# Attention weights summed over partitions by VectorE transpositions, and the first scores of an image spread evenly

## The chip, the cores and the metric

The kernel runs on one core of a Trainium2 chip. The metric is the time of one execution on the device, in microseconds (us); the time of a kernel is the median of its runs. TensorE (PE in the profile) multiplies matrices, VectorE (DVE) and ScalarE (ACT) work on tensors in SBUF and PSUM, GpSimd (POOL) on tensors in SBUF, and SyncE (SP) here issues transfers.

## The reference

Two layers on x of shape (4, 256, 64, 64) in float32. The first is attention over the 4096 positions of each image, with 32 channels for queries and keys:

```python
q = einsum('oc,bcn->bno', wq, xf) + bq
k = einsum('oc,bcn->bon', wk, xf) + bk[None, :, None]
attn = softmax(einsum('bnd,bdm->bnm', q, k), axis=-1)
v = einsum('oc,bcn->bon', wv, xf) + bv[None, :, None]
out = einsum('bcn,bmn->bcm', v, attn)
x = gamma[0] * out + x
```

The second layer is a cluster block: a group norm, a clustering of points around pooled centres with its own small projections, a second group norm, a two-layer perceptron with GELU (256 to 1024 to 256 channels), an affine step with ReLU, and a last 256 to 256 projection with ReLU. The change touches the attention alone.

## The kernel before, in words

The four images go one after the other. For each there are two long stages: `weighting` (the attention, some 525 us) and `cluster` with `mlp` (the second layer, some 328 us). The instructions of all engines are put out in one order written by hand, and each engine works through its own in that order.

In the attention an image's 4096 queries are cut into 8 blocks of 512 (`NBLK`), and for each block the 4096 keys into 8 groups of 512 (`GRP`). A pair of block `nb` and group `g` is a unit `u = 8 nb + g`; an image has 64 units. A unit goes through four steps:

- `score(u)` (L347): four float32 products give the scores of 512 keys by 512 queries, keys on the partitions, into the two double-bank PSUM tiles of `ps_s`. ScalarE copies both halves to SBUF (L377, L382) and VectorE takes running maxima of both (L381, L384; in the first group of a block L379 alone). Only two such tiles exist, so the next score waits until both have been read by both engines.
- `exps(u)` (L443): VectorE subtracts the maximum of each query (two instructions, L451), ScalarE takes the exponential (two, L454), GpSimd adds the weights to a running sum `acc` (two, L459; one, L456, for the first group).
- `weigh(u, av, quarter)` (L461), quarters 0 to 3: products of the weights with the values, accumulated over the block's eight units in the PSUM tiles `av`. These products at L464 fill most of TensorE's time. A float32 product shows as two records in the profile, so a quarter has 4 records and a unit 16.
- Once per block: `fold`, `highest` and `known` (the maximum of each query over the partitions, for the next block), `gather` (L473: the two halves of `acc` are added into `rdens`), `clear` (`av` is scaled out of PSUM), `total`, `add` (L498: GpSimd multiplies by the reciprocal sums and adds to the image), `seen` and `pooled` (statistics).

`highest` (L414) already gets from partitions to a row without TensorE: a VectorE transposition of 32 by 32 blocks (L417), a reduction (L420), four copies that bring the four groups of 32 partitions together (L423), a second reduction (L425), a small transposition (L428), and then `everywhere` (L81): one transfer of the row to HBM (L84) and one that reads it back to all 128 partitions (L85).

`total` (L483) does for the sums what `highest` does for the maxima, but with TensorE: four products with a matrix of ones (L488) give the sums on the partitions, VectorE takes the reciprocal of 128 by 128 numbers (L496), and the same two transfers spread them. It is called for block `nb - 1` in the first unit of block `nb`, between the products of quarters 1 and 2; seven times per image, 28 in all. The last block of an image has its own path (L645 to L672), which the change leaves alone.

What order the scores have against the products is in the table `at`, which maps (unit, quarter) to the unit whose scores come next. As a rule the scores of unit `u + 10` come at the start of unit `u` (`LEAD` is 10). For the second to fourth image, the first eight scores of its own stage have a rule of their own, since only units 0 to 7 have scores by then:

```python
at = {(u, 0): u + LEAD for u in range(units - LEAD)}
if b:
    for i in range(6):
        del at[i, 0]
    at.update({divmod(3 * i + 2, RG): GRP + i for i in range(8)})
```

Of the kernel before, what the change touches and what calls it, by code (L numbers as in the profile page):

```python
# [8 lines left out]
F32 = mybir.dt.float32  # L9
AF = mybir.ActivationFunctionType  # L10
ALU = mybir.AluOpType
AX = mybir.AxisListType

P = 128
# [3 lines left out]
NB = 512  # L18
NBLK = N // NB
XT = 1024  # L20
D = 32
# [7 lines left out]
RG, GRP = 4, N // NB  # L29
# [16 lines left out]
def attention_then_cluster_block(  # L46
# [17 lines left out]
    nc = tc.nc  # L64
# [7 lines left out]
    swap = ctx.enter_context(tc.tile_pool(name="swap", bufs=1))  # L72
# [4 lines left out]
    ps_m = ctx.enter_context(tc.tile_pool(name="ps_m", bufs=2, space=PSUM))  # L77

    dram = ctx.enter_context(tc.tile_pool(name="dram", bufs=2, space=bass.MemoryType.DRAM))

    def everywhere(dst, rows, shape, name):  # L81

        d = dram.tile([NB], F32, tag="row", name=f"row_{name}")
        nc.sync.dma_start(out=d.rearrange("(a b) -> a b", a=shape), in_=rows)  # L84
        nc.sync.dma_start(out=dst, in_=d.partition_broadcast(P))  # L85

    def load_x(b, t):
# [17 lines left out]
    for r in range(RG):  # L105
        nc.sync.dma_start(
            out=bqk_s[r * D : (r + 1) * D, :], in_=pv[:D, PV["bq"] : PV["bq"] + 2]
# [12 lines left out]
        out=pool_w[:, :, :16], in_=consts[:, K_POOL : K_POOL + P].rearrange("p (j s) -> p j s", j=8)  # L120
# [24 lines left out]
    ones = const.tile([P, P], F32, name="ones")  # L145
# [125 lines left out]
    def attention(b, xs):  # L271


        own = {}
        stats = small.tile([P, 2 * NBLK, 6], F32, tag="stats", name=f"st1_{b}")
        cells = small.tile([P, KC, NBLK, 4], F32, tag="cells", name=f"cells_{b}")
        qs, slots, mxs, accs, tops, rdens, ts = {}, {}, {}, {}, {}, {}, {}
# [128 lines left out]

        def spare():
            if "w2" not in own:
                own["w2"] = swap.tile([P, 3, P], F32, tag="w2", name=f"few_{b}")
                nc.gpsimd.memset(own["w2"], 0.0)  # L410
            return own["w2"]

        def highest(nb):

            top = tops.pop(nb)
            fl = top[:, 1]
            nc.vector.transpose(fl, top[:, 0])  # L417
            low = spare()[:, nb % 2]
            mx = low[:, :16]
            nc.vector.tensor_reduce(mx, fl.rearrange("p (c n) -> p c n", n=D), AX.X, ALU.max)  # L420
            four = low[:D, D : D + 64].rearrange("p (r c) -> p r c", r=4)
            for r in range(4):
                nc.vector.tensor_copy(four[:, r], mx[r * D : (r + 1) * D])  # L423
            one = low[:D, 3 * D : 4 * D]
            nc.vector.tensor_reduce(  # L425
                one[:, :16], low[:D, D : D + 64].rearrange("p (r c) -> p c r", r=4), AX.X, ALU.max
            )
            nc.vector.transpose(low[:D, :D], one)  # L428
            mb = work.tile([P, NB], F32, tag="w2", bufs=1, name=f"mr_{b}_{nb}")
            everywhere(mb, low[:16, :D], 16, f"mx_{b}_{nb}")  # L430
            return mb

        def known(nb, mb):
# [48 lines left out]

        def total(nb):  # L483


            den = ps_m.tile([P, NB], F32, tag="m", name=f"den_{b}_{nb}")
            for j in range(4):
                nc.tensor.matmul(  # L488
                    den[j * D : (j + 1) * D, :P],
                    ones[:, :D],  # L490
                    rdens[nb][:, j * P : (j + 1) * P],
                    start=True,
                    stop=True,
                )
            rec = spare()[:, 2]
            nc.vector.reciprocal(rec, den[:, :P])  # L496
            everywhere(rdens[nb], rec[::D], 4, f"rd_{b}_{nb}")

        def add(nb):
            t_s, rden = ts.pop(nb), rdens.pop(nb)  # L500
# [58 lines left out]
        at = {(u, 0): u + LEAD for u in range(units - LEAD)}  # L559
        if b:  # L560
            for i in range(6):
                del at[i, 0]
            at.update({divmod(3 * i + 2, RG): GRP + i for i in range(8)})
        else:
            at[0, 2], at[0, 0] = at[0, 0], GRP + 1

# [7 lines left out]
        def weighting(ahead, fill, early):  # L574
# [3 lines left out]
            for u in range(units):  # L578
# [29 lines left out]
                if nb:  # L608
                    if g == 0:
                        total(nb - 1)  # L610
                    elif g == 3:
                        add(nb - 1)
                    elif g == 5:
                        seen(nb - 1)
                    elif g == 7:
                        pooled(nb - 1)
# [5 lines left out]
                if g == GRP - 3 and more:  # L622
                    mb = highest(nb + 1)
# [724 lines left out]
    with tc.manual_schedule():  # L1348
        here = attention(0, xs0)
        here.alone()  # L1350
        late = None
        for b in range(B):
            xs1, begun = [], []
            nxt = attention(b + 1, xs1) if b + 1 < B else None

            def ahead():
                if nxt and len(xs1) < N // XT:
                    xs1.append(load_x(b + 1, len(xs1)))
                elif late and not begun:
                    begun.append(begin())  # L1360

            begin, todo, gelu = late or (None, list(nxt.projections) if nxt else [], lambda i: None)
            fill = filler(todo)
            stats, cells, rest = here.weighting(ahead, fill, (lambda: None) if b else derived)
            stats2 = cluster(b, here.xs, stats, cells, rest, fill, gelu)

            late = mlp(b, here.xs, stats2, fill, nxt, NBLK - (b == B - 2))
            here = nxt
# [76 lines left out]
```

## Time and profile before

| | |
|---|---|
| time, median of 3 runs | 3447.35 us (3444.46 to 3449.81) |
| span of the profiled execution | 3448.3 us |
| TensorE busy | 3390.0 us, 98% |
| VectorE busy | 2002.3 us, 58% |
| ScalarE busy | 1678.9 us, 49% |
| GpSimd busy | 1489.6 us, 43% |
| products of `total`, L488 | 224 records, median 285 ns each |
| products of `weigh`, L464 | 4096 records, 1831.5 us busy |
| products of `score`, L359 | 2048 records, 297.8 us busy |
| row of sums: transfer out, then back to all partitions | 1.3 us and 3.1 us to landing |

How to read it: the groups of instructions list, for each line and form, how often it ran, how long it was busy and what it waited for. Records of products overlap[...]; so a count times the mean of one overstates what they cost, and the chain of work that ended last, which gives every stretch of time to one piece of work, is the better measure of a cost in a stage that TensorE bounds. The waits list who sat idle for whom. The timeline gives start and length of single instructions, and shows how early a result is there before the engine that needs it asks for it.

### The profile page before, as it was taken

The numbers are of one execution on the slowest core, as the hardware profiler recorded it, in microseconds if no ns is written. First come the engines' busy times: TensorE is split into PE (matmuls) and PEld (weight loads), VectorE is DVE, ScalarE is ACT, GpSimd is POOL, SyncE is SP. The second block draws the span as 40 slices with busy tenths as digits, with TensorE's granted clock in tenths as the row PEclk, the third lists the DMA queues.
The fourth block names the chain that finished last, engine by engine and source line by source line (L and its number), as shares of the span: only waits on it lengthen the run. The fifth ranks groups of instructions, "written<-read, shape, count | busy, mean of one in ns | idle before, by whom it ended". The sixth has DMA issues, their size and how long they took to land.

```text
span 3448.3 us, 32176 instructions
## 1 busy us (share of the span) xinstructions
PE 3390.0 (98%) x11760; PEld 1673.2 (49%) x11760; DVE 2002.3 (58%) x2995; ACT 1678.9 (49%) x2157; POOL 1489.6 (43%) x807
## 2 busy tenths in 40 slices
PE   8999999999999999999999999999999999999999
PEld 4433445655433344565543343466553343446565
DVE  4666664645566666464456666646546666754543
ACT  5545543444555554344455555434445555543444
POOL 2665665211255666521125566652004566672200
PEclk9999999999999999999999999999999999999999
DMA  2000002000000000200000000020000000010000
GB/s 70 13 13 13 13 11 80 7 19 13 20 12 13 13 13 22 69 7 19 19 16 13 10 14 12 22 69 7 19 19 13 13 13 13 13 35 1 13 19 25
DMA packets 40829, 70.03 MB, mean 20 GB/s; under 512 B 8848, under 2 KB 16224, under 8 KB 40672
## 3 DMA queue, kind: packets, MB, share of 16 engines
q1 hardware_dynamic: 35808, 61.16, 5.4%
q10 hardware_dynamic: 4608, 6.30, 0.8%
q8 instruction: 93, 1.52, 0.2%
q14 instruction: 64, 0.52, 0.1%
q0 software_dynamic: 256, 0.52, 0.0%
HBM read 42.68 MB, written 16.89 MB: 17 GB/s over the span
## 4 chain that ended last, share of the span: by engine, by line
PE 94%; DVE 4%; ACT 1%; issue 1%; DMA 0%; SPq 0%; ACTq 0%; DVEq 0%
PE av L464 52%; PE mo L1202 12%; PE sc L359 8%; PE hu L1195 4%; PE pw L1171 3%; PE hp L1195 3%; PE hq L1195 3%; PE vp L310 2%; PE fv L857 2%; PE op L978 1%; PE qp L329 0%; PE kp L287 0%; PE agg L887 0%; DVE vf L866 0%; DVE hs L1231 0%
## 5 line engine op out<-in xcount | busy, mean ns | idle before, releaser
L464 PE MATMUL av<-s,v 128*128 128x512 f32 x4096 | 1831.5, 600 | 0.6 <-ACT s L454 0.6
L459 POOL TENSOR_TENSOR acc<-acc,s 128x1024 f32<-128x1024 f32 x448 | 1056.5, 2358 | 558.7 <-ACT s L454 539.7
L464 PEld LDWEIGHTS av<-s,v 128*128 128x128 f32 x4096 | 758.6, 190 | 1039.9 <-issue 1031.6
L454 ACT ACTIVATE s<-s 128x1024 f32<-128x1024 f32 x512 | 539.9, 1057 | 527.2 <-DVE s L451 486.1
L451 DVE TENSOR_TENSOR s<-s,mb 128x1024 f32<-128x1024 f32 x512 | 595.0, 1205 | 16.8 <-ACT mb L435 15.1
L381 DVE TENSOR_TENSOR top<-sc,top 128x1024 f32<-128x1024 f32 x196 | 239.8, 1223 | 473.5 <-PE sc L359 473.5
L1202 PE MATMUL mo<-hs,w 128*128 128x512 f32 x992 | 507.7, 595 | 3.8 <-ACT hs L1224 1.6
L1224 ACT ACTIVATE hs<-hs,pv_s 128x256 f32<-128x256 f32 x496 | 251.4, 508 | 359.9 <-DVE hs L1231 348.9
L1231 DVE TENSOR_TENSOR hs<-hu,hs 128x256 f32<-128x256 f32 x372 | 157.5, 423 | 355.4 <-ACT hs L1234 205.6
L377 ACT COPY s<-sc 128x1024 f32<-128x1024 f32 x224 | 225.3, 1006 | 283.9 <-PE sc L359 283.8
L1157 POOL TENSOR_TENSOR xn<-xn 128x256 f32<-128x256 f32 x27 | 23.9, 887 | 682.0 <-DVE xn L1144 459.8
L359 PE MATMUL sc<-q,k 32*128 32x512 f32 x2048 | 297.8, 640 | 6.8 <-ACT s L382 6.8
L384 DVE TENSOR_TENSOR top<-sc,top 128x1024 f32<-128x1024 f32 x196 | 240.0, 1225 | 50.4 <-ACT s L377 35.2
L382 ACT COPY s<-sc 128x1024 f32<-128x1024 f32 x224 | 227.0, 1013 | 71.6 <-DVE top L379 36.1
L456 POOL TENSOR_TENSOR acc<-s 128x1024 f32<-128x1024 f32 x32 | 75.3, 2353 | 364.2 <-ACT s L454 364.2
L1231 DVE TENSOR_TENSOR hs<-hq,hs 128x256 f32<-128x256 f32 x372 | 146.0, 420 | 107.1 <-PE hq L1195 102.9
L1202 PEld LDWEIGHTS mo<-hs,w 128*128 128x128 f32 x992 | 186.6, 190 | 42.5 <-ACT hs L1234 7.8
L359 PEld LDWEIGHTS sc<-q,k 32*128 32x128 f32 x2048 | 83.0, 183 | 199.9 <-issue 136.6
L1195 PE MATMUL hp<-xn,w 128*128 128x256 f32 x496 | 150.6, 385 | 2.6 <-ACT v L318 2.6
L1195 PEld LDWEIGHTS hp<-xn,w 128*128 128x128 f32 x496 | 92.4, 190 | 72.9 <-issue 62.4
L310 PE MATMUL vp<-wv_s,x 128*128 128x256 f32 x512 | 123.4, 387 | 0.2 <-ACT v L318 0.2
L1171 PE MATMUL pw<-xn,wpw_s 128*128 128x512 f32 x248 | 112.0, 594 | 3.4 <-ACT xn L1265 2.2
(219 smaller groups left out, 2696.7 us busy)
## 6 DMA issues: line engine op xcount, KB each, us to landing
x<-in_x SPq DMA_DIRECT2D x32, 512.0 KB, 5.8
out<-xn SPq DMA_DIRECT2D x62, 256.0 KB, 2.1
w<-in_w SPq DMA_DIRECT2D x8, 1024.0 KB, 9.7
mr<-row_mx SPq DMA_DIRECT2D x28, 256.0 KB, 3.1
rden<-row_rd SPq DMA_DIRECT2D x28, 256.0 KB, 3.1
q<-q ACTq DMA_DIRECT2D x96, 64.0 KB, 2.0
mix<-in_wfv SPq DMA_DIRECT2D x8, 192.0 KB, 4.9
q<-q SPq DMA_DIRECT2D x24, 64.0 KB, 2.0
```

Source lines behind the costliest of these rows:

```text
L359: nc.tensor.matmul(halves[r // 2][:, r % 2, :], k_s[rows, g, :], q_s[rows, :], start=True, stop=True)
L381: nc.vector.tensor_tensor(top, halves[1], top, ALU.max)
L382: nc.scalar.copy(s[:, 2:4, :], halves[1])
L384: nc.vector.tensor_tensor(top, halves[0], top, ALU.max)
L451: nc.vector.tensor_tensor(sh, sh, mxs[nb].unsqueeze(1).to_broadcast([P, 2, NB]), ALU.subtract)
L454: nc.scalar.activation(sh, sh, AF.Exp)
L459: nc.gpsimd.tensor_tensor(acc, acc, s[:, 2 * h : 2 * h + 2], ALU.add)
L464: nc.tensor.matmul(av[c], own["v"][:, RG * g + quarter, c * P : (c + 1) * P], slots[u][:, quarter, :], start=(g == 0 and quarter == 0), st ...
L1195: nc.tensor.matmul(out, w[:, j * P : (j + 1) * P], x, start=True, stop=True)
L1202: yield nc.tensor.matmul(acc[c], w2_s[:, jj, c * P : (c + 1) * P], hs[:, i], start=(j == 0 and i == 0), stop=(j == HID // P // 2 - 1 and i ...
L1224: nc.scalar.activation(dst, src, act, bias=bias)
L1231: nc.vector.tensor_tensor(dst, ps, term, ALU.add)
```

## The change

`total` gives up the four products and the PSUM tile. It sums over partitions as `highest` takes maxima: what both do is put into `reduced` (block transposition, reduction, four copies, second reduction; the operation is an argument) and `rows` (small transposition and the two transfers). The reciprocal is then taken of 32 by 16 numbers, ahead of the small transposition. The scratch tile of `spare` grows from three to seven parts for the transposed sums; only the first three are cleared, as before. The row of sums leaves from 16 partitions rather than 4. The purpose is to take this work off TensorE.

The second edit is to the table `at`: the first eight scores of the second to fourth image's stage come at quarters 2, 4, 7, 10, 13, 16, 18 and 21 of the stage rather than at 2, 5, 8, 11, 14, 17, 20 and 23. The next score after them is at quarter 24 in both. The purpose is to have no two scores closer than two quarters.

```diff
-    def everywhere(dst, rows, shape, name):
+    def everywhere(dst, rows, name):
         d = dram.tile([NB], F32, tag="row", name=f"row_{name}")
-        nc.sync.dma_start(out=d.rearrange("(a b) -> a b", a=shape), in_=rows)
+        nc.sync.dma_start(out=d.rearrange("(a b) -> a b", b=D), in_=rows)
         nc.sync.dma_start(out=dst, in_=d.partition_broadcast(P))
...
-                own["w2"] = swap.tile([P, 3, P], F32, tag="w2", name=f"few_{b}")
-                nc.gpsimd.memset(own["w2"], 0.0)
+                own["w2"] = swap.tile([P, 7, P], F32, tag="w2", name=f"few_{b}")
+                nc.gpsimd.memset(own["w2"][:, :3], 0.0)
...
+        def reduced(src, flipped, low, op):
+            nc.vector.transpose(flipped, src)
+            nc.vector.tensor_reduce(
+                low[:, :16], flipped.rearrange("p (c n) -> p c n", n=D), AX.X, op
+            )
             four = low[:D, D : D + 64].rearrange("p (r c) -> p r c", r=4)
             for r in range(4):
-                nc.vector.tensor_copy(four[:, r], mx[r * D : (r + 1) * D])
+                nc.vector.tensor_copy(four[:, r], low[r * D : (r + 1) * D, :16])
             one = low[:D, 3 * D : 4 * D]
             nc.vector.tensor_reduce(
-                one[:, :16], low[:D, D : D + 64].rearrange("p (r c) -> p c r", r=4), AX.X, ALU.max
-            )
+                one[:, :16], low[:D, D : D + 64].rearrange("p (r c) -> p c r", r=4), AX.X, op
+            )
+            return one
+
+        def rows(one, low, dst, name):
             nc.vector.transpose(low[:D, :D], one)
+            everywhere(dst, low[:16, :D], name)
...
         def total(nb):
-            den = ps_m.tile([P, NB], F32, tag="m", name=f"den_{b}_{nb}")
-            for j in range(4):
-                nc.tensor.matmul(
-                    den[j * D : (j + 1) * D, :P],
-                    ones[:, :D],
-                    rdens[nb][:, j * P : (j + 1) * P],
-                    start=True,
-                    stop=True,
-                )
-            rec = spare()[:, 2]
-            nc.vector.reciprocal(rec, den[:, :P])
-            everywhere(rdens[nb], rec[::D], 4, f"rd_{b}_{nb}")
+            few = spare()
+            low = few[:, 2]
+            flipped = few[:, 3:].rearrange("p a n -> p (a n)")
+            one = reduced(rdens[nb], flipped, low, ALU.add)
+            nc.vector.reciprocal(one[:, :16], one[:, :16])
+            rows(one, low, rdens[nb], f"rd_{b}_{nb}")
...
-            at.update({divmod(3 * i + 2, RG): GRP + i for i in range(8)})
+            at.update({divmod((14 * i + 10) // 5, RG): GRP + i for i in range(8)})
```

## The prediction

> **What bounds the kernel now.** I read the page first: the busy time of the engines and the chain of work that ended last.
>
> ```profile
> PE 3390.0 (98%) x11760; PEld 1673.2 (49%) x11760; DVE 2002.3 (58%) x2995; ACT 1678.9 (49%) x2157; POOL 1489.6 (43%) x807
> PE 94%; DVE 4%; ACT 1%; issue 1%; DMA 0%; SPq 0%; ACTq 0%; DVEq 0%
> ```
>
> TensorE is busy for 98% of the span and holds 94% of the chain. So work taken off TensorE counts in full as long as nothing else then makes it wait, and work put on VectorE (58% busy) counts only where it makes TensorE wait. What is worth asking is what the four sums cost TensorE, where it idles, and how much time VectorE has around them. For the first, the chain in order of time around the first sums of the first image:
>
> ```profile
> 134.40 3.63 PE av L464 x8
> 138.03 0.36 PE den L488 x8
> 138.39 3.63 PE av L464 x8
> 142.02 1.07 PE sc L359 x8
> 143.09 7.06 PE av L464 x16
> ```
>
> The columns are start, length and work; in a timeline a bracket gives the idle time before and who ended it. The sums hold 0.36 us of the chain, and their mean of 285 ns times 8 records (2.28 us) would be six times too much. But the unit that they split takes 3.63 + 3.63 = 7.26 us for its 16 products where the next takes 7.06: breaking the run of products costs another 0.20 us. The distance between the starts of successive scores says the same: 142.02 - 133.33 = 8.69 us with the sums, 150.15 - 142.02 = 8.13 without, 0.56 us more. The same distances stand around the sums of another image (987.26, 995.95, 1004.08 in the timeline).
>
> For the second, the chain through the first eight units of the second image, from its first products at 915.28 to the products of its unit 7:
>
> ```profile
> 963.64 1.14 PE sc L359 x8
> ...
> 977.44 1.13 PE sc L359 x4
> 978.57 1.83 PE av L464 x2
> ```
>
> Between the first two lines the chain leaves TensorE: it goes over VectorE's maxima of the score at 963.64, the fold and `highest`, the subtraction, and ScalarE's exponential and copies, and only comes back with the second half of the score at 977.44. The cause is in the table of scores: quarters 23 and 24 each have one, one quarter of products apart. For the price I add up the stretch as if TensorE had not waited, from pieces of the same answer: the first 8 products 3.43, seven runs of 12 at 5.35 = 37.45, a run of 4 at 1.92 (a run of n costs 0.20 + 0.43 n, which fits 3.63, 5.35 and 7.06), a run of 16 at 7.06, ten scores at 1.07 = 10.70. That is 60.56 us; it took 978.57 - 915.28 = 63.29. So 2.73 us are lost. The waits name only 0.50 + 0.78 = 1.28 us of it (for ScalarE's copy L382); the rest sits inside records that were issued and then stood. The third and fourth image show the same 63.29 (1770.69 to 1833.98, 2601.27 to 2664.56). The first image has no such rule and no such wait.
>
> **What the Trainium skill says.** "VectorE: DVE Perf Modes", section "The three transpose paths": VectorE transposes only blocks of 32 by 32. That is why the change needs four copies across groups of 32 partitions and a second reduction; the trace has the same sequence in `highest`, so I take its durations and not the page's. "PSUM — Partial Sum Buffer", section "PSUM bank collisions raise a hardware error": two engines must not touch one bank and quadrant at a time, two readers included. The trace agrees: ScalarE's copy L382 waits 0.25 us for VectorE's L381 on the same half, and L384 waits for L377. So each score is given back only after two rounds, which matters for the replay below. "TensorE: Matmul & The Clock Gate", section "Part 3: Packing small matmuls": products in different column groups run at the same time. The sums use four column groups, and 8 records of 285 ns in 0.36 us agree.
>
> **The change part by part.** Removed from TensorE: 28 times 0.56 = 15.6 us (bounds: 0.36 if the 0.20 stays behind elsewhere, 10.1 us, to 0.56).
>
> Added to VectorE, from these groups of instructions (busy time, then mean of one in ns):
>
> ```profile
> L496 DVE RECIPROCAL few<-den 128x128 f32<-128x128 f32 x28 | 26.6, 949 | 4.2 <-PE den L488 4.2
> L417 DVE STREAM_TRANSPOSE top<-top 128x512 f32<-128x512 f32 x28 | 19.5, 696 | 0.1
> L420 DVE TENSOR_REDUCE few<-top 128x16 f32<-128x512 f32 x28 | 19.2, 686 | 1.2
> L423 DVE COPY few<-few 32x16 f32<-32x16 f32 x112 | 18.3, 164 | 2.1
> L425 DVE TENSOR_REDUCE few<-few 32x16 f32<-32x64 f32 x28 | 6.9, 248 | 1.0
> L428 DVE STREAM_TRANSPOSE few<-few 32x32 f32<-32x32 f32 x28 | 5.6, 199 | 1.0
> ```
>
> New per block: 0.696 + 0.686 + 4 x 0.164 + 0.248 + 0.199 = 2.49 us, and a reciprocal of 16 columns. That size is not in the trace; reciprocals of 1 and 64 columns take 160 and 553 ns, so 16 columns lie between, and on the line 160 + 6.24 x 15 = 0.25 us (bounds 0.16 to 0.55). Sum 2.74, less 0.95 for the old reciprocal: 1.8 us more busy. With the gaps that the sequence shows in `highest` (1034.12 to the next subtraction at 1036.71, 2.59 us) and 0.28 for the reciprocal, the stretch is 2.87 us where the old one was 0.86 (993.54 to 994.40): VectorE comes 2.0 us later to what follows, 56 us over 28 blocks, 1.6% of the span.
>
> Does that reach TensorE? Behind the sums on VectorE stand the subtractions for the next unit but one, then the maxima of the next score; ScalarE's exponentials wait for the first, and its copies stand behind these. TensorE waits for two things: weights and a free score tile. From the timeline of the second image:
>
> ```profile
> 993.54 0.95 DVE L496 RECIPROCAL few<-den 128x128 f32<-128x128 f32 x1
> 994.40 2.28 DVE L451 TENSOR_TENSOR s<-s,mb 128x1024 f32<-128x1024 f32 x2
> 995.95 1.14 PE L359 MATMUL sc<-q,k 32*128 32x512 f32 x8
> 998.71 1.22 DVE L384 TENSOR_TENSOR top<-sc,top 128x1024 f32<-128x1024 f32 x1 [0.30 <-ACT s L377]
> 1004.08 1.14 PE L359 MATMUL sc<-q,k 32*128 32x512 f32 x8
> ```
>
> Replayed 2.0 later: subtractions from 996.4 to 998.7, exponentials to 999.8, L381 to 999.9, copies L377 to 1000.8 and L382 to 1001.8, L384 to 1002.0. The next score now wants the tile at 1004.08 - 0.56 = 1003.5: 1.5 us to spare. Those exponentials are needed only by the products behind that score, 4.8 us later. After that score VectorE has caught up: in the old timeline it idles 3.12 us before the maxima that follow. So I cost the added 56 us of VectorE at nothing; a longer reciprocal (0.55) would still leave 1.2 us.
>
> The new first instruction reads `rdens`, which GpSimd's `gather` has written at 979.3, 14 us before: no new wait. The row of sums leaves 2.0 us later, after 996.4, and takes 1.3 and 3.1 us to land plus issue, so it is back near 1001.3; GpSimd asks for it at 1014.97. The larger scratch tile, the freed PSUM tile and the row from 16 partitions (as the row of maxima has it) have nobody waiting on them.
>
> The scores: with the new quarters the stretch costs, by the same pieces, 3.43 + 2 x 3.63 + 6 x 5.35 + 7.06 + 10.70 = 60.55 us if nobody waits. The replay of it, score by score: where two quarters lie between (quarters 2 to 4, and 16 to 18) the next score comes 4.7 us after the one before it. The first pair is the tightest: the score at 918.71 is read out by L382 at 923.2, as in the trace, and its tile's second half is wanted near 923.9. The second pair: score at 949.1, L384 to 952.9, wanted at 953.8. The score at quarter 21 (960.2) is read by 963.8, `highest` ends at 967.3, the exponentials of unit 7 at 970.6, wanted at 975.8; the next unit's first score, at 966.6, is off its tile at 973.9, wanted at 974.8. So no wait is left, and 3 x 2.73 = 8.2 us come back (bounds: 3 x 1.28 = 3.8 if only the named waits do).
>
> Sum: 15.6 + 8.2 = 23.8 us, and 3447.35 - 23.8 = 3423.6 us.
>
> **The rivals.** One: the gain is partial. The 0.20 us stays where other work splits the products, or the closer pairs of scores wait for ScalarE as the old pair did: 10.1 + 3.8 = 13.9 us, 3433.4. For it speaks that the margin of the first pair is only 0.7 us; against it, that the distances between scores measure the 0.56 directly.
>
> Two: the wait moves. VectorE's 2.0 us per block uses more than the 1.5 us to spare, by about what is saved, and TensorE waits some 0.8 us per block: 28 x 0.8 = 22.4, 3446. This needs my replay to be 1.3 us too early.
>
> Three, slower: VectorE sets the pace at the start of each block, so all of its 2.0 us show: 28 x 2.0 = 56 against 23.8 gained, +32, 3480. For it speaks only that the chain does run over VectorE where two scores lie close; against it, VectorE's idle time of 473.5 us before L381, for scores from TensorE.
>
> **How the numbers follow.** Forecast as worked out 0.72, rival one 0.16, two 0.06, three 0.06. The time is that of the first case. For the range I add the scatter of the time before (3 us) below, 3420, and on the other side take in rival one and its scatter, 3437; rivals two and three, 0.12, stay outside. Faster by over 0.2% (under 3440.5): 0.88. Same: 0.06. Slower: 0.06.
>
> **What would show it right or wrong.** In the changed kernel successive scores around the new sums lie 8.13 us apart, like their neighbours; the second image goes from its first products to those of unit 7 in 60.6 us; TensorE has no wait for L382 or L384 after the sums; VectorE's busy time grows by about 50 us; and GpSimd's `add` has no wait for the row of sums. A wait of TensorE on the score tile two scores after a block begins would make rival two or three true. A stretch above 62 us at the start of an image would say that the even spacing only moved the wait.

## The result, and the profile after

The changed kernel takes 3418.46 us (median of 4 runs, 3414.81 to 3419.37) against 3445.9 us for the kernel before: a ratio of 0.9918, 95% interval 0.9901 to 0.9935. Five later runs gave 3418.48 us and 0.9914 (0.9900 to 0.9928). It is faster, as forecast, but by more: the forecast was 23.8 us less and a range that ended at 3420.0. In the mean the two kernels are 28.3 us apart in the first comparison (four runs of each) and 30.3 us in the second (26 runs of the kernel before, five of the changed one).

The page of the changed kernel, busy time and chain:

```profile
PE 3363.0 (98%) x11536; PEld 1663.4 (49%) x11536; DVE 2069.2 (61%) x3219; ACT 1674.2 (49%) x2157; POOL 1490.3 (44%) x807
PE 95%; DVE 3%; ACT 1%; issue 0%; DMA 0%; SPq 0%; ACTq 0%; DVEq 0%
```

TensorE still bounds it. VectorE has 67 us more and holds less of the chain than before. The chain around the place where the first sums stood:

```profile
133.90 1.07 PE sc L359 x8
134.97 7.06 PE av L473 x16
142.04 1.07 PE sc L359 x8
143.11 7.07 PE av L473 x16
150.17 1.07 PE sc L359 x8
```

The unit that took 8.69 us takes 8.14, as its neighbour does. In the first image, where only this part acts, the stretch from the maximum's transposition to the next group norm is 533.11 us where it was 537.03: 3.92 us less, 7 x 0.56. The chain through the first units of the second image, whose products begin at 912.00:

```profile
956.92 1.07 PE sc L359 x8
957.99 5.35 PE av L473 x12
963.34 1.07 PE sc L359 x8
964.41 7.07 PE av L473 x16
971.48 1.07 PE sc L359 x8
972.55 3.63 PE av L473 x8
```

It no longer leaves TensorE, and 972.55 - 912.00 = 60.55 us, the forecast to the last digit. The fourth image takes the same. In the third the score of quarter 28 stands 0.23 us (1.30 us in the chain and not 1.07), because ScalarE's copy L382 of the score before it ends late; in the second image that copy ends only 0.17 us before TensorE starts this score, so the replay's 0.9 us to spare was too much. With the spacing alone the third image loses nothing there, so it comes with VectorE's added work. The margin behind the sums is as replayed, as the timeline of the second image shows:

```profile
985.82 0.70 DVE L415 STREAM_TRANSPOSE few<-rden 128x512 f32<-128x512 f32 x1
988.85 2.30 DVE L460 TENSOR_TENSOR s<-s,mb 128x1024 f32<-128x1024 f32 x2
993.17 1.22 DVE L384 TENSOR_TENSOR top<-sc,top 128x1024 f32<-128x1024 f32 x1 [0.89 <-ACT s L377]
995.81 0.71 PE L359 MATMUL sc<-q,k 32*128 32x512 f32 x4
```

The sums hold VectorE for 3.03 us (2.87 forecast), and the score tile is free at 994.4, 1.4 us before TensorE wants it (1.5 forecast). So the steps that were priced came out, but for those 0.23 us. What was missing stands in the chain of the kernel before, just behind the stretch that the prediction looked at, whose last line was cut off by the end of the window. The chain goes on, and the busy time in four stretches (the number before the last two is the granted TensorE clock) says why:

```profile
977.44 1.13 PE sc L359 x4
978.57 8.76 PE av L464 x16
987.33 1.07 PE sc L359 x8
```

```profile
core 0: us, PE busy (x) PEld busy (x) DVE busy (x) ACT busy (x) POOL busy (x), PEclk, DMA share, GB/s
970.00:975.00 5.00, 5.00 (x13) 2.15 (x12) 3.00 (x6) 2.93 (x3) 1.80 (x1) 1.00 0.16 53
975.00:978.00 3.00, 2.22 (x10) 0.60 (x8) 1.22 (x1) 1.71 (x4) 2.91 (x2) 1.00 0.00 0
978.00:982.00 4.00, 4.00 (x9) 1.44 (x6) 3.28 (x3) 2.87 (x3) 1.27 (x1) 0.59 0.00 0
982.00:986.00 4.00, 4.00 (x11) 1.85 (x10) 1.43 (x2) 2.11 (x2) 1.34 (x1) 0.98 0.00 0
```

The 16 products of unit 7 take 8.76 us and not 7.06: behind the wait the granted clock is one half for 3.4 us, and the wait costs 2.73 + 1.70 us. The fourth image has the same, the third has not. The Trainium skill, "TensorE: Matmul & The Clock Gate", section "What's actually happening", says that the clock is throttled by how busy the array has been, judged in windows of about 3.4 us that run freely. The traces agree with the windows: the half-clock stretches inside them are 3.4 us long, or 6.8, or in one case 10.2, and in each trace they start whole steps of 3.413 us apart. In the trace of before three of them start at 634.0, 978.7 and 1487.3 us, which is 101 and 149 such steps. These steps are called the grid below. They do not follow the program: in four traces of the kernel before, the same wait of the second image ended 0.2 to 0.3 us ahead of a grid point three times and 0.1 us behind one the fourth time.

### The profile page after: what moved, and what is told of

Read it like the earlier page. It is cut to its first block, busy times and chain, and to the rows that moved or that the text cites. A ratio compares the mean times of both kernels' runs of the same rounds, so it can differ in the third digit from the quotient of the medians.

```text
span 3417.5 us, 31890 instructions
## 1 busy us (share of the span) xinstructions
PE 3363.0 (98%) x11536; PEld 1663.4 (49%) x11536; DVE 2069.2 (61%) x3219; ACT 1674.2 (49%) x2157; POOL 1490.3 (44%) x807
## 4 chain that ended last, share of the span: by engine, by line
PE 95%; DVE 3%; ACT 1%; issue 0%; DMA 0%; SPq 0%; ACTq 0%; DVEq 0%
PE av L473 53%; PE mo L1204 12%; PE sc L359 8%; PE hu L1197 4%; PE pw L1173 3%; PE hp L1197 3%; PE hq L1197 3%; PE vp L310 2%; PE fv L859 2%; PE op L980 1%; PE qp L329 0%; PE kp L287 0%; DVE vf L868 0%; DVE hs L1233 0%; PE agg L889 0%
## 5 line engine op out<-in xcount | busy, mean ns | idle before, releaser
L382 ACT COPY s<-sc 128x1024 f32<-128x1024 f32 x224 | 227.0, 1014 | 66.2 <-DVE top L379 36.1
## 6 DMA issues: line engine op xcount, KB each, us to landing
w<-in_w SPq DMA_DIRECT2D x8, 1024.0 KB, 10.2
```

The costliest lines, as they stand in the source:

```text
L382: nc.scalar.copy(s[:, 2:4, :], halves[1])
```

## The experiments

All but the last three traces have the kernel before measured on the same chip: 16 runs with a mean of 3446.4 us and a mean clock of 0.9947 for the sums alone, the spacing alone, the last score moved and the products moved, and 26 runs with 3448.15 us and 0.9942 for the other four. The nine runs of the changed kernel have a mean of 3417.85 us at 0.9964. Runs of one kernel differ most by the granted clock that they happened to get (of the 26, those at 0.993 take 3451.7 us in the mean, those at 0.996 take 3442.4), so the mean clock of a kernel's runs stands with its time.

**The sums alone.**

```diff
-            at.update({divmod((14 * i + 10) // 5, RG): GRP + i for i in range(8)})
+            at.update({divmod(3 * i + 2, RG): GRP + i for i in range(8)})
```

> The changed kernel with the old quarters for the first scores (2, 5, ... 23): only the sums change. Theory (three terms): 28 x 0.56 = 15.6 us less than before, about 3430; the three waits of 2.73 us stay, and after some of them TensorE runs at half clock, so the distance from the last of these scores to the next block's score stays above 8.2 us in some images. Rival A (the sums were sized too low, the spacing was right at 8.2): 27.4 - 8.2 = 19.2 us less, about 3427. Rival B (the sums give only their own 0.36): 10 us less, 3436.

Measured 3431.91 us (5 runs, mean 3432.6, clock 0.9946); ratio 0.9962 (0.9949 to 0.9974). In the mean that is 13.8 us under the kernel before at the same clock, where the sums were forecast at 15.6. The interval, 9 to 18 us, holds the forecast, leaves out rival A and just holds rival B; the distances between scores leave out B: 8.13 and 8.14 us where the sums were, 0.56 less than before, in every image. The three waits are there as before (3.56, 8.41 and 10.03 us between the starts of the last scores of the second image's stretch, as in the kernel before without half clock), and two of the three are followed by half clock.

**The spacing alone**, the opposite edit on the kernel before.

> The kernel before with only the new quarters. Theory: the three waits of 2.73 us go, and with them the half-clock stretches that followed two of the three in the trace of before (1.69 us each): 8.2 to 13.3 us less, middle 11.6, about 3434. Rival A (only the waits go): 8.2 less, 3438. Rival C (only the waits that the profile names): 3.8 less, 3442. In the trace the mean granted clock over the 4 us behind unit 7's first products is 1.00 in all images.

Measured 3435.34 us (5 runs, mean 3435.4, clock 0.9960); ratio 0.9970 (0.9958 to 0.9982), 11.0 us under the mean of before. Theory's middle was 11.6; the interval, 6 to 14 us, leaves out rival C but holds rival A's 8.2 too. In the trace the stretch is 2.73 us shorter in all three images and none has half clock behind it. The two halves give 13.8 + 11.0 = 24.8 us where both edits together gave 28.3 and 30.3. By the forecast of the work they should give 23.8; the rest of this section looks for what lies between. The mean clocks make a table of their own: 0.9947 before and 0.9946 with the sums alone, 0.9960 with the spacing alone, 0.9964 with both. Among these four the better clock comes with the spacing, but an experiment below gets it with the old quarters.

**Only the last score moved.** Of the eight quarters only 23 becomes 22.

```diff
-            at.update({divmod((14 * i + 10) // 5, RG): GRP + i for i in range(8)})
+            at.update({divmod(min(3 * i + 2, 22), RG): GRP + i for i in range(8)})
```

> The changed kernel, but of the eight quarters only the last one differs from the old list (22 in place of 23). If the wait comes only from the two scores one quarter apart, two quarters are enough and this is as fast as the changed kernel, within 2 us of 3418. Rival: the chain over the fold, highest and the exponential of unit 7 starts 1 quarter (1.8 us) later than in the changed kernel, where it had 5 us to spare, so that can not matter, but the score at quarter 24 is read late and the one at quarter 28 waits again: part of the 2.73 us per image stays, 3 to 8 us slower than the changed kernel.

Measured 3423.33 us (6 runs, mean 3423.6, clock 0.9957), 5.7 us more in the mean than the changed kernel, which was not run beside it: the rival. In the timeline of the second image the score of quarter 28 stands:

```profile
963.64 1.14 PE L359 MATMUL sc<-q,k 32*128 32x512 f32 x8
964.71 7.13 PE L473 MATMUL av<-s,v 128*128 128x512 f32 x16
971.77 2.17 PE L359 MATMUL sc<-q,k 32*128 32x512 f32 x8
973.87 7.13 PE L473 MATMUL av<-s,v 128*128 128x512 f32 x16
```

It takes 2.17 us and not 1.14: 1.03 us are lost in the second and the fourth image and 1.38 in the third, 3.4 us in all. That is 3.2 more than in the changed kernel; the rest goes with the lower clock. So two quarters between scores are enough for the score itself, but `highest` and the exponential of unit 7 sit behind the last of them, and the score after next pays. What the new list gives is a full quarter more for that chain; its other shifted quarters were not tried one by one.

**The products moved beside the score**, in the kernel before.

```diff
+                if nb and g == 0:
+                    total(nb - 1)
                 if u or b:
                     weigh(u, av, 0)
                     due(u, 1)
                     weigh(u, av, 1)
                 if nb:
-                    if g == 0:
-                        total(nb - 1)
-                    elif g == 3:
+                    if g == 3:
                         add(nb - 1)
```

> The kernel before, with the four products of the sums moved from between quarters 1 and 2 to directly behind the score that opens the unit, where the run of products is broken anyway. Theory (0.36 for the products, 0.20 for breaking the run): 28 x 0.20 = 5.6 us less than before, 3440; scores around the sums are 8.49 us apart. Rival: the whole 0.56 belongs to the products wherever they stand: no change.

Measured 3437.62 us (10 runs, clock 0.9959); ratio 0.9976 (0.9967 to 0.9985), 8.7 us under the mean of before where 5.6 was expected. The chain has the expected 5.6 (28 x 0.20), since the run of 16 is whole again:

```profile
132.79 1.07 PE sc L359 x8
133.86 0.36 PE den L488 x8
134.21 7.06 PE av L464 x16
141.28 1.07 PE sc L359 x8
```

The scores are 8.49 us apart in place of 8.69, so the 0.20 us belongs to the broken run. The rest is clock, 0.9959 against 0.9947 (0.0012 x 3446 = 4.1 us): this trace has none of the half-clock stretches behind the three waits, though the waits are there. So a clock as good as that of the spacing alone came with the old quarters.

**The products done twice**, in the kernel before.

```diff
-            for j in range(4):
+            for j in (0, 1, 2, 3) * 2:
```

> The kernel before with the four products of each sum done twice in a row. Theory: only their own 0.36 is paid again, not the broken run: 28 x 0.36 = 10.1 us slower than before; scores around the sums 9.05 us apart. Rival: every group of these products costs 0.56: 15.7 us slower, 9.25 apart.

Measured 3450.09 us (13 runs, mean 3450.1, clock 0.9955), 2.0 us over the mean of before, with an interval of the ratio from 0.9998 to 1.0014: neither answer. The time alone is inconclusive, since these runs also got a better clock than those of before, worth 0.0013 x 3448 = 4.5 us. The chain gives the size: 16 records in 0.57 us where 8 took 0.36, and the scores 8.91 us apart, 0.22 more.

```profile
134.27 1.07 PE sc L359 x8
135.34 3.63 PE av L464 x8
138.97 0.57 PE den L488 x16
139.55 3.63 PE av L464 x8
143.18 1.07 PE sc L359 x8
```

So both expectations were too high. Of the 0.56 us that one group costs, 0.22 us is its own stream, 0.14 us comes once with the group, and 0.20 us is the broken run.

**VectorE's sums done twice**, in the changed kernel.

```diff
+            reduced(rdens[nb], flipped, low, ALU.add)
             one = reduced(rdens[nb], flipped, low, ALU.add)
```

> The changed kernel with the reduction of each sum (transposition, reduction, four copies, second reduction) done twice, about 2.6 us more of VectorE in each of 28 blocks. Theory: 1.4 us of it fit before the score after next wants its tile, so TensorE waits about 1.2 us per block: 34 us slower than the changed kernel, and up to 20 us more if half-clock stretches follow these waits as often as the ones at the start of an image. Rival A (VectorE is free): no change. Rival B (nothing is to spare): 73 us slower.

Measured 3441.51 us (14 runs, mean 3441.2, clock 0.9952), 23.3 us over the changed kernel on the same chip. Neither rival; the theory's direction, with fewer waits than its 34 us. In the timeline the wait comes where it was expected, at the second score after the sums:

```profile
1001.60 1.02 ACT L382 COPY s<-sc 128x1024 f32<-128x1024 f32 x1
1001.74 1.22 DVE L384 TENSOR_TENSOR top<-sc,top 128x1024 f32<-128x1024 f32 x1 [0.89 <-ACT s L377]
1002.67 1.47 PE L359 MATMUL sc<-q,k 32*128 32x512 f32 x8 [0.57 <-ACT s L382]
```

That score is 8.76 us behind the one before it and the next 8.47, so 0.63 + 0.34 us are lost in this block. The four attention stages are longer by 5.6, 4.8, 4.6 and 5.0 us, 20.0 in all, 0.71 per block: VectorE was given 2.5 us more per block and TensorE felt 0.7, so some 1.8 us were free, a little more than the replay said. The other 3.3 us go with the lower clock. None of these short waits is followed by half clock in the trace.

**Three more products ahead of the counts**, in the changed kernel. They are taken from later fillings of the second layer to close a wait of 2.7 us there.

```diff
         gelu(1)
-        fill(3)
+        fill(6)
```

> The changed kernel with three more of the next image's products put into the gap where TensorE waits 2.7 us for the one-hot weights ahead of the counts in the second layer, taken from later fillings. If half-clock stretches there come from this wait, they go, and with the gap itself it is up to 2.7 + 1.7 us per image, 10 to 17 us faster than the changed kernel. Rival: the wait only moves to where the three products were taken from: within 3 us, and half-clock stretches move with it.

Measured 3429.28 us (5 runs, mean 3429.8, clock 0.9926), 11.9 us slower than the changed kernel on the same chip, worse than its rival allowed. The waits of TensorE, by total, first without and then with the edit:

```profile
PE cnt L910 <- DVE scr L829: 9.9, 4, 2.7
PE gnm_gn L241 <- DVE mv_gn L239: 3.8, 4, 3.2
```

```profile
PE gnm_gn L241 <- DVE mv_gn L239: 10.1, 6, 3.2
PE pwl L1097 <- ACT xl L1085: 6.4, 2, 4.9
PE hp L1197 <- issue: 5.5, 3, 1.8
```

The wait for the counts is gone, and larger ones stand where the products were taken. The half-clock stretches moved with them and grew: in the second layer they add up to 44.2 us where the changed kernel has 20.4. Half of the difference is 11.9 us, as much as the whole loss, and the mean clock fell from 0.9964 to 0.9926. So this is no better version, and the changed kernel stays the best.

**The changed kernel again**, the base for the last two experiments on it.

> The changed kernel itself, as the base for the others on the same chip and to pin the gain: 25 to 29 us less than before. By terms: 28 x 0.56 = 15.7 for the sums, 3 x 2.73 = 8.2 for the waits, and 4/9 x 3 x 1.7 = 2.3 for half-clock stretches behind those waits (they followed 4 of 9 such waits in the traces so far): 26.2. Rival: the terms that were forecast, 23.8, are all and the rest was scatter: 22 to 25.

Measured 3418.48 us (5 runs, mean 3417.9, clock 0.9964): 30.3 us under the mean of before, more than both expected. The part that was still too small is the clock, as the sums at equal clock below show, and that is what the last runs are for.

**The kernel before, three more traces.**

> The kernel before, for another trace. Its 26 runs so far lie between 3442 and 3452 us, and the longer ones have the lower mean granted clock (0.996 at 3442, 0.993 at 3452). Theory: a run near 3443 has no half-clock stretch behind the three waits at the start of an image, a run near 3451 has two or three, and stretches of 3.4 or 6.8 us in the second layer make up the rest. Rival: the waits at the start of an image are followed by half clock about as often in short runs as in long ones, and only the second layer differs.

> As the trace before it: the same kernel, the same two theories.

> As the two traces before it: the same kernel, the same two theories.

They came out at 3452.13, 3451.77 and 3444.29 us. Spans and clocks of the first and the third:

```profile
core 0: 3450.3 us, clock 0.993
core 0: 3442.5 us, clock 0.995
```

And the busy time of the two in 4 us around the end of the same wait, in the second image (the third number from the end is the clock):

```profile
980.00:984.00 4.00, 4.00 (x9) 1.43 (x6) 3.27 (x3) 2.88 (x3) 1.28 (x1) 0.60 0.00 0
```

```profile
978.00:982.00 4.00, 3.56 (x10) 1.55 (x11) 2.28 (x2) 3.87 (x5) 2.25 (x2) 1.00 0.00 0
```

In the two long runs the wait is followed by half clock in the second and fourth image, in the short one in none: the theory. The waits themselves are the same length in all three. In the second layer the long runs have half-clock stretches of 3.4, 6.8, 6.8, 3.4, 3.4 and 6.8 us (30.6) where the short one has 3.4, 3.4, 6.8, 3.4 and 6.8 (23.8). With the two of 3.4 us behind the waits they differ by 13.6 us of half clock; a stretch at half clock loses half its length, so that is 6.8 us lost, of the 7.8 and 7.5 between the long times and the short one.

## Why the prediction was wrong

- **The sums, 15.6 us**: right. The distances between scores show 0.56 us less in every block; the sums alone gave 13.8 us in the time, with an interval of 9 to 18.
- **VectorE's added work at nothing**: right. 1.4 us were to spare where 1.5 had been replayed, and doubling that work brought 0.7 us of wait per block; what it cost is the 0.23 us of the third image. Its size was too small: VectorE has 66.9 us more and not 50. The transpositions, reductions and the new reciprocal (241 ns) are as priced; the 224 copies average 235 ns and not 164, which is the missing 224 x 0.071 = 16 us.
- **The waits, "3 x 2.73 = 8.2 us come back"**: the waits did go, but for 0.23 us in the third image. This is the step that failed, by a term that it put at nothing without a word: it priced the idle time and not the clock that TensorE gets behind it, and left the clock of the rest as it was. The line that shows it was in the chain of before: 8.76 us for 16 products that take 7.06. In place of nothing, the clock brought some 5 to 7 us.
- **How much the clock gave.** What the order of work gives can be read where the clock is the same. From the first to the last product of `weigh`, the four attention stages without half clock behind the wait are shorter by 3.9, 6.6, 6.4 and 6.6 us (the first image from the trace of before, 520.69 to 516.77 us; the others from the trace at 3444.29, which has 518.78 in each, to 512.17, 512.40 and 512.17). That is 23.5 us, against the forecast of 23.8. Where runs of both kernels have the same mean clock, 0.996, the kernel before takes 3442.4 us (3 runs) and the changed one 3419.3 (5 runs): 23.1 us. The other 7.2 us of the 30.3 come with the clock, 0.9942 to 0.9964 in the mean, which is 0.0022 x 3448 = 7.6 us of full clock. Directly behind the three waits, half clock followed 9 of 21 in seven traces with the old quarters (those of before, of the sums alone and of the two edits of the products), which makes 9/21 x 3 x 1.7 = 2.2 us per run; with the even quarters it followed in none of 15 images. The other 5 us lie in the second layer.
- **What decides the clock behind a wait.** It is the wait's place on the grid of 3.413 us, taken for each trace from its own half-clock stretches. The 2.7 us waits ahead of the counts in the first three images show it: there are 36 in the twelve traces that have them. Half clock for 3.4 us followed the 21 that ended 1.58 to 3.12 us behind a grid point, for 6.8 us the nine that ended within 0.17 us ahead of one or up to 0.55 us behind it, and none followed the six that ended 0.74 to 1.09 us behind one. At the start of an image, eight of the nine waits with half clock ended 0.19 to 0.55 us ahead of a grid point (the ninth, where the stretch was 0.4 us longer, 0.10 us behind one); the twelve without ended 0.59 to 1.65 us ahead or 0.05 to 0.08 us behind.
- **What stays open.** How often a kernel's waits come to lie in each place is not shown, since the runs without a trace do not tell. So the clock's part of the gain is measured, but not shown to belong to the spacing, beyond the 2.2 us of waits that no longer exist: with the products only moved, the old quarters had 0.9959. Any edit that shifts later work by a part of 3.4 us can change it, and to that extent it was luck.
- **The range.** Its lower end took 3 us for the scatter, from three runs of the kernel before. The 26 runs reach from 3442.1 to 3452.2 us. With the 2.2 us of clock behind the waits the forecast would have been 26.0 us less, 3421.4.
- **The rivals**: none came true. No wait of their size took the place of the old ones, and the spacing didn't stop at a part of the gain. That a part would have been lost with two quarters and no more is what the third experiment shows.

## What to carry to other kernels

When a wait of the engine that bounds a kernel is to be removed, read the granted clock in the few microseconds behind it, and compare the length of the work there with the same work elsewhere: the wait may cost more than its idle time, and not in every run, since where it falls on the grid decides. Where runs of a kernel scatter by more than the effect that is looked for, compare runs with the same mean clock; here that brought 30.3 us down to 23.1, where the order of work explains 23.5. And a short group of products in the middle of a long run costs more than its own stream, so its place is worth as much thought as its length.

## What the hardware showed unexpectedly

Of the four small copies of a sum, one or two take longer beside GpSimd. The copies of a maximum, the same instructions, take 161 to 167 ns in the kernel before, where GpSimd is idle at 1035.56 in the second image, for one; those of the sums stand where GpSimd adds weights: the first of the four takes some 0.30 us in 24 of 28 blocks, and once per image the first takes 1.1 and the third 2.2. All copies of the changed kernel, and then the timeline of the longest in the first image:

```profile
L421 DVE COPY few<-few x224: 161/164/2228, 115.5 to 3045.4; 32x16 f32<-32x16 f32 x112
```

```profile
526.85 4.78 POOL L468 TENSOR_TENSOR acc<-acc,s 128x1024 f32<-128x1024 f32 x2 [4.33 <-ACT s L463]
528.12 3.70 DVE L421 COPY few<-few 32x16 f32<-32x16 f32 x4
531.86 0.25 DVE L423 TENSOR_REDUCE few<-few 32x16 f32<-32x64 f32 x1
```

The first copy ends at 529.23 and the third at 531.65, each 0.02 us behind the end of one of GpSimd's two additions. The transposition and the reduction at the same place are not slower (702 and 686 ns). The Trainium skill, "SBUF — State Buffer", section "Who interferes with whom", says that VectorE's copies can use a pair of ports that it shares with GpSimd, and that whoever comes second waits for a whole instruction; these ends agree, though no run here moved the copies. It cost no time: at that place, in the last block of an image, no score waits for VectorE.
